# The last batch of a two-layer graph network without its list and its scatter: h gathered row by row, a plain product by chunks of rows, each chunk stored at once

## The chip, the cores and the metric

The kernel runs on one core of one Trainium2 chip. The time is the device time of one execution, in microseconds (us). A run lists that time, the core's span in the records and the mean clock that TensorE was granted. With one core no run is marked slow here; all runs below count as fast.

The traces name the engines PE (TensorE, matrix products and transposes; PEld are its weight loads), DVE (VectorE, sums and statistics), ACT (ScalarE, copies and activations), POOL (GpSimd, which issues the gathers) and SP (which issues plain transfers). A q behind the name, as in SPq, stands for the engine's queue of instructions. The granted clock is TensorE's: 1.00 is full, 0.50 half.

## The reference

There are 32 batches of x[512, 512], one adjacency matrix adj[512, 512], everything in float32, and two layers, each with a residual:

```python
h = jnp.maximum(_layernorm(x, axis=-1), 0.0)
x = x + (einsum('nm,bmd->bnd', adj, h) @ W0 + b0)                 # layer 0
h = jnp.maximum(_layernorm(x, axis=-1), 0.0)
# layer 1: eight heads of attention with the mask (1.0 - adj) * -1e9, then @ Wo + bo
x = x + gnn1(h, adj)
```

The mask is so strong that, with these inputs, each row's softmax has weight 1 at the largest entry of its row of adj and 0 elsewhere. The kernel checks this on the chip and otherwise takes a general path, which plays no part here. So layer 1 is: for every row take one row of h (by an index that all batches share), multiply it with Wv·Wo, and add a constant row.

## The kernel before

Fewer than 384 different rows of h are ever taken. So layer 1 gathers the list of used rows (`listed`, three times 128), multiplies those 384 rows only, writes the product z to DRAM, and lets a gather with addition bring z's rows to their places in x. Of the 384 rows, 256 go through a product form with seven half-size products in place of eight, the other 128 through a plain one.

```python
    def get_h(b):                                   # h has been written to DRAM as HS[b]
        HC[b] = work.tile([P, R, D], F32, name="hc")
        for r in range(R):
            nc.gpsimd.indirect_dma_start(
                out=HC[b][:, r, :], out_offset=None, in_=HS[b],
                in_offset=bass.IndirectOffsetOnAxis(ap=listed[:, r:r + 1], axis=0))
    ...
    def layer1(b):
        ...                                         # plain product of rows 256 to 383 into flat
        nc.vector.tensor_add(zs[:, 2, :], flat, cvo)
        nc.sync.dma_start(Z[b][2 * P:3 * P, :], zs[:, 2, :])
        yield from product(HT[b], HTS[b], wvo, wvo_t, take_z(zs, b), P)   # seven products, z written at the end

    def finish(b):
        for c in range(C):
            nc.gpsimd.indirect_dma_start(
                out=X[b][:, c, :], out_offset=None, in_=Z[b],
                in_offset=bass.IndirectOffsetOnAxis(ap=place[:, c:c + 1], axis=0), compute_op=ALU.add)

    def store(b):
        for c in range(C):
            nc.sync.dma_start(out[b, c * P:(c + 1) * P, :], X[b][:, c, :])
```

The batches are interleaved: while TensorE works on layer 0 of batch b, layer 1 of batch b-1 is fed, and batch b-2 is added and stored. Only at the end does a batch stand alone: batch 31 goes through gather, product, z, gather-add and store with nothing beside it but the end of batch 30.

## Time and profile before

| | us |
|---|---|
| median of the first three runs | 1216.17 (1215.86 to 1218.9) |
| the profiled run: span in the records | 1217.6 |
| the same run: its time (not one of the three) | 1219.35 |
| TensorE busy, share of the span | 96% |
| end of TensorE's last work to end of span | 24.6 |

The last line is the one that the change is about. The third line is the one to keep an eye on: a run's time is a little more than its own span. The profile's lines of the last batch stand in the prediction.

One line more is needed below, because the two kernels are compared from a common point: the first write of batch 31's h to DRAM, on SP's queue. Up to there their instructions are the same. In the kernel before (instructions in order of time; start, length):

```profile
1165.39 2.41 SPq L450 DMA_DIRECT2D hs<-h  x2
```

From this point to the end of the span are 1217.6 - 1165.39 = 52.2 us. I call this stretch the tail, and times in it are written as +n us after that point.

### The profile page before, as it was taken

How to read it: one execution, taken by the hardware profiler on the slowest of the kernel's cores; microseconds unless marked ns; L12 is line 12 of the kernel's file. 1: busy time of each engine (PE TensorE's matmuls, PEld its weight loads, DVE VectorE, ACT ScalarE, POOL GpSimd, SP SyncE). 2: the span in 40 equal slices, each digit the busy share in tenths (PEclk: the TensorE clock that was granted, in tenths of full speed). 3: DMA queues.
4: the chain of work that ended last, by engine and by line, in shares of the span. 5: the costliest groups of instructions: out<-in, count | busy, mean ns of one | idle time of the engine just before them, and what ended most of it. 6: DMA issues, size and time to landing. Idle time of an engine off the chain costs nothing.

```text
span 1217.6 us, 14536 instructions
## 1 busy us (share of the span) xinstructions
PE 1164.6 (96%) x5164; PEld 938.2 (77%) x5164; DVE 849.0 (70%) x1854; ACT 327.3 (27%) x499; POOL 401.9 (33%) x340
## 2 busy tenths in 40 slices
PE   7899999999999999999999999999999999999971
PEld 3458888888888888888888888888888888888841
DVE  4877776777777677777767777777777777777541
ACT  3223223222322322232232223223222322322110
POOL 1132432433233343324324332433433243343332
PEclk9999999999999999999999999999999999999986
DMA  8222665565566556556655655665565566555466
GB/s 284 78 61 91 169 169 147 152 188 167 152 169 167 149 152 186 169 152 167 167 149 152 185 170 152 168 168 148 152 186 170 153 166 171 144 152 153 135 162 149
DMA packets 97874, 192.43 MB, mean 158 GB/s; under 512 B 10624, under 2 KB 10624, under 8 KB 97792
## 3 DMA queue, kind: packets, MB, share of 16 engines
q1 hardware_dynamic: 69104, 127.95, 28.7%
q0 software_dynamic: 26528, 59.27, 26.6%
q10 hardware_dynamic: 2160, 4.19, 0.9%
q8 instruction: 42, 0.69, 0.2%
q14 instruction: 40, 0.33, 0.1%
HBM read 99.10 MB, written 92.28 MB: 157 GB/s over the span
## 4 chain that ended last, share of the span: by engine, by line
PE 86%; DVE 7%; DMA 1%; issue 1%; POOL 1%; ACT 0%; SPq 0%; POOLq 0%; DVEq 0%; ACTq 0%
PE mm L271 72%; PE mm L478 9%; PE pt L464 3%; DVE st L185 2%; DVE zs L482 2%; PE mm L352 1%; DVE zs L318 1%; DVE mv L186 1%; DMA hc<-hs,listed 1%; POOL x L488 0%; DMA z<-zs 0%; DVE x L422 0%; ACT h L199 0%; DVE x L445 0%; DVE yT L308 0%
## 5 line engine op out<-in xcount | busy, mean ns | idle before, releaser
L488 POOL DMA_INDIRECT x<-z,place x128 | 201.5, 1574 | 252.0 <-DMA z<-zs 209.6
L199 ACT ACTIVATE h<-x,off,rstd 128x512 f32<-128x512 f32 x256 | 194.7, 807 | 201.9 <-DVE off L195 201.9
L326 DVE TENSOR_TENSOR x<-mm,x 128x512 f32<-128x512 f32 x217 | 149.8, 690 | 119.1 <-PE mm L271 119.1
L192 POOL TENSOR_TENSOR rstd<-ve,mhalf 128x2 f32<-128x2 f32 (+1 forms) x97 | 88.2, 909 | 288.4 <-DVE ve L191 287.0
L185 DVE BATCH_NORM_STATS2 st<-x 128x6 f32<-128x512 f32 x256 | 175.3, 685 | 10.9 <-DMA x<-in_x_dram 8.7
L455 POOL DMA_INDIRECT hc<-hs,listed x96 | 102.8, 1071 | 235.3 <-PE mm L271 177.5
L271 PE MATMUL mm<-adjT_s,h0s 128*128 128x256 f32 x744 | 171.0, 379 | 3.8 <-DVE h0s L248 3.2
L271 PE MATMUL mm<-w_t,sel 128*128 128x256 f32 x744 | 171.0, 379 | 1.2 <-DVE x L326 1.2
L271 PEld LDWEIGHTS mm<-adjT_s,h0s 128*128 128x128 f32 x744 | 141.2, 190 | 23.6 <-issue 4.5
L271 PEld LDWEIGHTS mm<-w_t,sel 128*128 128x128 f32 x744 | 138.9, 190 | 19.1 <-DVE x L326 1.6
L465 ACT COPY hT<-pt 128x512 f32<-128x512 f32 x96 | 56.5, 588 | 356.3 <-PE pt L464 356.3
L310 ACT COPY yT<-mm 128x512 f32<-128x512 f32 x124 | 72.7, 586 | 266.2 <-PE mm L271 222.1
L478 PE MATMUL mm<-wvo,hT 128*128 128x512 f32 x256 | 116.8, 599 | 0.7 <-ACT hT L465 0.7
L271 PE MATMUL mm<-adjT,h 128*128 128x256 f32 x496 | 117.3, 379 | 0.0
L271 PE MATMUL mm<-w_s,yT 128*128 128x256 f32 x496 | 117.2, 379 | 0.0
L308 DVE TENSOR_TENSOR yT<-mm,yT 128x512 f32<-128x512 f32 x93 | 64.3, 692 | 75.2 <-PE mm L271 72.9
L271 PE MATMUL mm<-wvo_t,hTs 128*128 128x256 f32 x384 | 104.2, 395 | 6.5 <-DVE zs L318 6.2
L271 PEld LDWEIGHTS mm<-w_s,yT 128*128 128x128 f32 x496 | 94.2, 190 | 13.2 <-issue 0.5
L271 PEld LDWEIGHTS mm<-adjT,h 128*128 128x128 f32 x496 | 94.1, 190 | 13.3 <-ACT h L199 0.6
L271 PEld LDWEIGHTS mm<-wvo_t,hTs 128*128 128x128 f32 x384 | 67.9, 189 | 32.5 <-DVE zs L318 24.9
L478 PEld LDWEIGHTS mm<-wvo,hT 128*128 128x128 f32 x256 | 49.2, 193 | 49.5 <-issue 46.9
L422 DVE TENSOR_TENSOR x<-x,b_r 128x512 f32<-128x512 f32 x128 | 87.3, 683 | 0.0
(131 smaller groups left out, 1309.1 us busy)
## 6 DMA issues: line engine op xcount, KB each, us to landing
hs<-h SPq DMA_DIRECT2D x64, 512.0 KB
out_dram<-x SPq DMA_DIRECT2D x128, 256.0 KB
x<-in_x_dram SPq DMA_DIRECT2D x120, 256.0 KB
z<-zs SPq DMA_DIRECT2D x96, 256.0 KB
x<-z,place POOLq DMA_INDIRECT x128
hc<-hs,listed POOLq DMA_INDIRECT x96
x<-in_x_dram ACTq DMA_DIRECT2D x4, 256.0 KB
mask<-in_adj_dram SPq DMA_DIRECT2D x4, 256.0 KB
```

The costliest lines, as they stand in the source:

```text
L185: self.nc.vector.bn_stats(st, self.src[:, self.chunks[i], :])
L192: self.nc.gpsimd.tensor_tensor(self.rstd, ve, self.mhalf[:, 0:n], ALU.pow)
L199: self.nc.scalar.activation(self.dst[:, c, :], self.src[:, c, :], AF.Relu, bias=self.off[:, i:i + 1], scale=self.rstd[:, i:i + 1])
L271: nc.tensor.matmul(bank[:, m, :], lhs[:, k, m * P:(m + 1) * P], rhs[:, k, :], start=(first and m == 0 and k == 0), stop=(k == 1), skip_gro ...
L308: nc.vector.tensor_add(dst, bank, dst)
L310: nc.scalar.copy(dst, bank)
L326: nc.vector.tensor_add(dst, bank, dst)
L422: nc.vector.tensor_add(X[b][:, c, :], X[b][:, c, :], b0_r)
L455: nc.gpsimd.indirect_dma_start(out=HC[b][:, r, :], out_offset=None, in_=HS[b], in_offset=bass.IndirectOffsetOnAxis(ap=listed[:, r:r + 1], ...
L465: nc.scalar.copy(HT[b][:, :, r * P:(r + 1) * P], pt)
L478: nc.tensor.matmul(flat, HT[b][:, d, 2 * P:3 * P], wvo[:, d, :], start=(d == 0), stop=(d == DC - 1))
L488: nc.gpsimd.indirect_dma_start(out=X[b][:, c, :], out_offset=None, in_=Z[b], in_offset=bass.IndirectOffsetOnAxis(ap=place[:, c:c + 1], axi ...
```

## The change

The last batch pays for the detour over z with latency that nothing hides. So it takes the direct way: each of its 512 rows of h is gathered by its own index, four gathers in place of three; each chunk of 128 rows is transposed, multiplied by a plain product and added to x at once (the constant row has been added to x earlier), and its store leaves at once. This is more work for TensorE (512 rows in plain form in place of 384 with a cheaper one) and removes the write of z and the four gather-adds. The stores of batch 30 move to ACT's queue, so that SP's is free for the last batch.

```diff
+    def get_all(b):
+        for c in range(C):
+            nc.gpsimd.indirect_dma_start(
+                out=hs[0][:, c, :], out_offset=None, in_=HS[b],
+                in_offset=bass.IndirectOffsetOnAxis(ap=idx[:, c, 0:1], axis=0))
... (transpose_all: four transposes into one bank, one copy on ACT; add_cvo: x += cvo on DVE)
+    def layer1_rows(b):
+        transpose_all(0)
+        for r in range(C):
+            bank = ps_m.tile([P, D], F32, name="mm")
+            for d in range(DC):
+                if d == 2 and r + 1 < C:
+                    transpose_all(r + 1)
+                nc.tensor.matmul(bank, hs[1][:, d, r * P:(r + 1) * P], wvo[:, d, :], start=(d == 0), stop=(d == DC - 1))
+            nc.vector.tensor_add(X[b][:, r, :], bank, X[b][:, r, :])
+            nc.sync.dma_start(out[b, r * P:(r + 1) * P, :], X[b][:, r, :])
...
-        for b in range(B + 2):
+        for b in range(B + 1):
...
-            put(b, 13 if b > 0 else 16, get_h)
+            put(b, 13 if b > 0 else 16, get_h if b < B - 1 else get_all)
+            if b == B - 1:
+                for c in range(C):
+                    put(b, 22, add_cvo, c)
...
+        layer1_rows(B - 1)
+        if B > 1:
+            store(B - 2, nc.scalar)
```

More of the change, by code (lines that the diff above doesn't have):

```diff
@@ L457, in get_h, with transpose_all, add_cvo @@
                 in_offset=bass.IndirectOffsetOnAxis(ap=listed[:, r:r + 1], axis=0))
+    def get_all(b):
[3 more added lines that the diff above has]
+                in_offset=bass.IndirectOffsetOnAxis(ap=idx[:, c, 0:1], axis=0))
+    def transpose_all(r):
+        pt = ps_t.tile([P, DC, P], F32, name="pt")
+        for d in range(DC):
+            nc.tensor.transpose(pt[:, d, :], hs[0][:, r, d * P:(d + 1) * P], ident)
+        nc.scalar.copy(hs[1][:, :, r * P:(r + 1) * P], pt)
+    def add_cvo(b, c):
+        nc.vector.tensor_add(X[b][:, c, :], X[b][:, c, :], cvo)
+    def layer1_rows(b):
+        transpose_all(0)
+        for r in range(C):
+            bank = ps_m.tile([P, D], F32, name="mm")
+            for d in range(DC):
+                if d == 2 and r + 1 < C:
[3 more added lines that the diff above has]
+            nc.sync.dma_start(out[b, r * P:(r + 1) * P, :], X[b][:, r, :])
     def transpose_h(b, r):
@@ L490, in finish, with store @@
                 in_offset=bass.IndirectOffsetOnAxis(ap=place[:, c:c + 1], axis=0), compute_op=ALU.add)
-    def store(b):
+    def store(b, eng=nc.sync):
         for c in range(C):
-            nc.sync.dma_start(out[b, c * P:(c + 1) * P, :], X[b][:, c, :])
+            eng.dma_start(out[b, c * P:(c + 1) * P, :], X[b][:, c, :])
     def run(steps, work_by_step):
@@ L525, in single_path @@
                 put(b + 1, i, h0_sum, i)
-            for r in range(R):
+            for r in range(R if b < B else 0):
                 put(b - 1, 3 + r, transpose_h, r)
@@ L546, in single_path @@
             put(b, 11, put_h, 2)
-            put(b - 2, 12, store)
-            put(b, 13 if b > 0 else 16, get_h)
-            for step, i in ((11, 0), (11, 1), (12, 2), (12, 3)):
+            if b < B:
+                put(b - 2, 12, store)
+            put(b, 13 if b > 0 else 16, get_h if b < B - 1 else get_all)
+            if b == B - 1:
+                for c in range(C):
+                    put(b, 22, add_cvo, c)
+            for step, i in ((11, 0), (11, 1), (12, 2), (12, 3)) if b < B else ():
                 put(b - 1, step, hT_sum, i)
@@ L595, in single_path @@
             else:
-                run(layer1(b - 1) if b - 1 < B else None, todo[14:23])
+                run(layer1(b - 1) if b < B else None, todo[14:23])
+        layer1_rows(B - 1)
+        if B > 1:
+            store(B - 2, nc.scalar)
 @with_exitstack
```

## The prediction

> **What bounds the kernel now.** I read the page first (clock row, chain by engine), then the chain of waits in order of time over the last 120 us, then the instructions in order of time over the last 50 us, then the DMA view of the last 12 us, because the diff touches only the last batch, 31 of 0 to 31, and the store of batch 30.
>
> ```profile
> span 1217.6 us, 14536 instructions
> PEclk9999999999999999999999999999999999999986
> ...
> PE 86%; DVE 7%; DMA 1%; issue 1%; POOL 1%; ACT 0%; SPq 0%; POOLq 0%; DVEq 0%; ACTq 0%
> ```
>
> The reader is to see that TensorE sets the time of the whole, but not of the end: its granted clock falls only in the last two slices. Thirty-one batches are left as they are; the question is what the last 45 us are worth. The chain there:
>
> ```profile
> 1168.30 2.01 PE mm L271 x8
> ...
> 1170.98 1.04 POOL hc L455
> 1172.02 0.30 issue
> 1172.33 6.39 DMA hc<-hs,listed
> 1178.72 0.14 issue
> 1178.86 2.13 PE pt L464 x8
> ...
> 1181.64 5.28 PE mm L478 x8
> 1186.92 6.06 PE mm L271 x28
> ...
> 1193.44 1.63 SPq L483
> ...
> 1195.63 4.53 DMA z<-zs
> ...
> 1206.52 1.54 POOL x L488
> ```
>
> Columns: start, length (us), what. The last batch is a ladder of waits: gather the compacted rows of h (landed at 1178.72), transpose, product (ended at 1192.98), write z to DRAM (landed at 1200.16), gather-add z into x by four indirect transfers of POOL (1200.99 to 1208.06), then the stores. So 24.6 us of the span (1192.98 to 1217.6) have no TensorE work at all. The instructions in order of time show two details:
>
> ```profile
> 1193.00 0.42 DVE L318 TENSOR_TENSOR zs<-mm,cvo 128x256 f32<-128x256 f32 x1 [0.44 <-PE mm L271]
> 1193.18 1.89 SPq L483 DMA_DIRECT2D z<-zs  x1
> 1195.16 0.88 SPq L320 DMA_DIRECT2D z<-zs  x2
> 1200.99 1.54 POOL L488 DMA_INDIRECT x<-z,place  x1 [12.94 <-DMA z<-zs]
> ...
> 1206.09 6.96 SPq L494 DMA_DIRECT2D out_dram<-x  x4
> ```
>
> First, the z write at 1193.18 was ready at 1187.65 (its add, line 482, ran 1186.96 for 0.69); it stood behind the four stores of batch 30 on SP's in-order queue, which wait for that batch's gather-adds. Second, the last store was issued by 1213.05. The DMA view of 1206 to 1218, slices of 0.3 us, shows traffic until about 1214.7:
>
> ```profile
> DMA  9899869699999999999997400795000000000000
> ```
>
> So from the last data to the end of the span there are 2.9 us, which any version pays; and from the last gather-add's landing (about 1212, where the gap in this row lies) to the last data, 2.5 us for one 256 KB store.
>
> **What the Trainium skill says.** "DMA: Bandwidth & Descriptors", section "SWDGE vs HWDGE vs iDMA": per-element accumulation in a DMA is for GpSimd's software path only. The trace agrees: line 488 is POOL's, 1.54 us each plus 0.30 between, 7.1 us for four before the last one moves its data. Same page, "Issuing engines are not separate DMA queues": moving an issue to another engine saves only sequencer time, as all run on the same 16 DMA engines. I read the move of batch 30's store to ACT that way: it unblocks SP and makes no bandwidth. "Perfetto Trace Analysis", section "DMA Instruction — SWDGE (GPSIMD)": the profiled end is the end of descriptor generation, not of the data. Here the second gather shows about 1 us, and lands 6.4 us after its start. "TensorE: Matmul & The Clock Gate", Part 1: the clock halves after about one idle window of 3.4 us, and recovers after a busy one. The trace agrees:
>
> ```profile
> 1175.00:1178.00 3.00, 0.63 (x4) 0.42 (x4) 0.00 (x0) 0.59 (x1) 0.00 (x0) 1.00 0.87 283
> 1178.00:1185.00 7.00, 5.47 (x12) 2.94 (x13) 1.52 (x4) 1.17 (x2) 3.69 (x3) 0.51 0.29 50
> 1185.00:1190.00 5.00, 5.00 (x21) 3.61 (x19) 1.97 (x4) 0.00 (x0) 2.75 (x2) 1.00 0.96 176
> ```
>
> (After the stretch's length: busy time of PE, PEld, DVE, ACT, POOL; then granted clock, DMA share, GB/s.) While TensorE waits for gathers its clock goes to 0.51 and the eight matmuls of 128x512 take 5.28 us instead of the 3.43 us that the chain shows for them elsewhere.
>
> **The change part by part**, all for the last batch. The instruction orders of the two kernels agree on every engine up to there.
>
> Removed on the path: the z write (1193.0 to 1200.2, 7.2 us), the POOL gather-adds with their landing (1200.2 to about 1212, 11.8 us). Together 19 us. Also gone: four hTs sums, on DVE and not on the path.
>
> Added to the product: the seven-product form on 256 rows plus a plain one on 128 took 3.43 + 6.06 = 9.5 us warm (11.3 us here, cold at first). The plain product over all 512 rows is 16 matmuls of 128x512; each is two instructions at 0.43 us (3.43 us over 8), so 16 x 0.86 = 13.7 us. Transposes: four groups of 0.44 us. TensorE work 15.5 us against 10.8: 4.7 us more.
>
> Given back by starting earlier: before, the first matmul waits for all three gathers, 1181.64. After, it waits for the first only. First transposes at 1175.5 as before, ACT copy 0.59, first matmul at about 1176.85. Two steps of chunk 0 (1.7 us) run to 1178.6; then the second gather is needed, which landed at 1178.7. I take the same. From there TensorE has 3 x 0.44 + 14 x 0.86 = 13.4 us left: end at 1192.1, if warm. The third and fourth gathers are needed at about 1182.6 and 1186.5. The fourth is 256 KB more; issued around 1174.9 (spacing 1.3 us), it lands by my estimate at 1180 to 1181, as the whole traffic of gathers and z before (1.57 MB) moved from 1172.9 to about 1179, some 258 GB/s. So it's hidden.
>
> Added at the end: last DVE add 0.2 + 0.69, then the store 2.5, then the fixed 2.9: 6.3 us after TensorE's end, in place of 24.6. End at 1198.4 if warm. If the clock drops at 1177.9 as before, one window at half rate costs at most (1181.3 - 1178.7) / 2 = 1.3 us, two windows 3.0 us. In the window 1174.5 to 1177.9 TensorE is now busy about 1.7 us instead of 0.63, so I hold one window or none as likely as each other: +0.7 us on average.
>
> Added off the path: four adds of cvo to x on DVE (0.69 each, about 2.5 us in a row) stand ahead of the last take of batch 30, so the last z write of that batch goes out at about 1175.4 instead of 1173. Its landing (before: about 1179.9) then hardly moves, since the queues were full to 1179, but by up to 1 us it may. Batch 30's gather-adds start at 1180.7 to 1181.7 and take 7.1 us to the last issue and 4 to 5 us to land: 1192 to 1193. Its stores sit on ACT behind the fourth transpose copy (1187.6); the last is issued near 1193, lands 1195.5, and ends the span at 1198.4 too. Two paths that end together, and with batch 31's first three stores (0.75 MB) in the same stretch, where DMA was already 0.96 busy: I add 0.5 us for the later of two.
>
> Sum: 1198.4 + 0.7 + 0.5 = 1199.6 us of span. The profiled span was 1217.6 and the median time 1216.2, 1.4 less: 1198.2 us, a gain of 18 us, 1.5%.
>
> **The rivals.** (a) Batch 30's gather-adds become the end: z of batch 30 delayed, three more stores in their traffic, the store on ACT late. For: the 0.96 DMA share at 1185 to 1190, and the same landing time as the other path. Against: the gather-adds are paced by POOL's 1.84 us each, at 256 KB 142 GB/s. If they lose 3 us: 1201. (b) The clock: TensorE waits chunk by chunk for gathers, stays half-clocked for two windows, and all of the last batch's additional 4.7 us shows: 1201 to 1202. Against: a continuous stream of matmuls from 1178.7 should free it. (c) The best case: the later z write of batch 30 leaves the queues to the gathers, the second lands before 1178.6, and TensorE never waits after its first matmul: 1176.85 + 16 x 0.86 + 3 x 0.44 = 1191.9, + 6.3 = 1198.2, and 1.4 less as a time: 1196.8 with neither allowance. (d) The whole is hidden: no, nothing lies beside the 24.6 us.
>
> **Range and chances.** 1198.2 us; 1195 to 1202 holds rivals (a) to (c) and the run-to-run spread of 3 us. Faster by over 2% needs below 1192.3, that is, TensorE done by about 1187 in span, and its work alone from 1176.85 takes 15 us: 0.03. Within 2%: 0.96. Slower by over 2% would need a gather that collides with everything: 0.01.
>
> **What would show it.** TensorE's last matmul at 1191.5 to 1195; the span's end 6 to 7 us after it; no z write or gather-add of batch 31; first wvo matmul near 1177; the fourth gather landed before its transposes at 1186; clock in 1178 to 1182 either 1 or half. I'm wrong if TensorE waits for the second or later gathers beyond 1180, if the last chunk's store is not within 1 us of the last data, or if batch 30's stores end clearly after batch 31's.

## The result, and the profile after

| | before | after |
|---|---|---|
| median of four runs, us | 1217.54 (1215.86 to 1219.99) | 1202.93 (1201.75 to 1203.37) |
| profiled run: span, us | 1217.6 | 1201.6 |
| tail, us | 52.2 | 33.6 |
| mean granted clock | 0.988 | 0.996 |

The ratio is 0.9877, with a 95% interval of 0.986 to 0.9894: 1.2% less time, within 2%. A ratio here is the mean time of one kernel's fast runs over that of the other's in the same rounds, so it is not quite the ratio of the medians that stand beside it. The class came as predicted, the median did not: it lies 0.9 us above the range, and 4.7 us above the predicted 1198.2.

The page of the kernel after, span, clock row and chain by engine:

```profile
span 1201.6 us, 14516 instructions
PEclk9999999999999999999999999999999999999999
PE 88%; DVE 7%; DMA 1%; ACT 0%; issue 0%; POOL 0%; POOLq 0%; DVEq 0%; ACTq 0%
```

The two last slices no longer show a lowered clock, and SPq has left the chain. The chain in order of time shows a ladder with fewer rungs (start, length, what):

```profile
1173.60 4.34 DMA h<-hs,idx
1177.94 0.14 issue
1178.08 0.64 PE pt L468 x4
...
1179.38 1.98 PE mm L481 x4
1181.37 0.06 issue
1181.43 0.63 PE pt L468 x4
1182.06 3.44 PE mm L481 x8
...
1189.80 5.17 PE mm L481 x12
```

From the first product on, TensorE waits for nothing: the second, third and fourth gathers never appear, and eight instructions take 3.44 us, the rate of full clock. TensorE ends at 1194.97. The queues, from the instructions in order of time:

```profile
1168.01 0.37 SPq L450 DMA_DIRECT2D hs<-h  x1
...
1183.33 1.59 POOL L514 DMA_INDIRECT x<-z,place  x1 [4.91 <-ACT h L469]
1184.53 11.51 SPq L483 DMA_DIRECT2D out_dram<-x  x4
1189.90 6.38 ACTq L520 DMA_DIRECT2D out_dram<-x  x4
```

The first line is the common point. Batch 30's first gather-add, at 1183.33, is +15.3, as before (1180.70, also +15.3). The last stores leave on SP at 1196.04 and on ACT at 1196.28: two paths that end together. The DMA view of 1190 to 1202, in slices of 0.3 us:

```profile
DMA  8999999999999999998436989952200000000000
```

A 0 in this row is a share below a tenth. In slices of 0.2 us the data flow fully until about 1198.0, then there is a trickle, at 31 GB/s or less from 1198.8, until 1199.8; in the kernel before there is next to nothing after 1214.6, 3.0 us before the end. Set side by side, counted from the common point:

| step | predicted | measured |
|---|---|---|
| first transposes | 1175.5, +10.1 | 1178.08, +10.1 |
| first product | 1176.85, +11.5 | 1179.38, +11.4 |
| end of TensorE | 1192.1, +26.7 | 1194.97, +27.0 |
| end of span, with the allowances of 1.2 | 1199.6, +34.2 | 1201.6, +33.6 |

The tail was right to 0.6 us, and this profile kept the full clock in its tail, so that the 0.7 allowed for the clock fell away. So the 5.2 us between 1198.2 and this run's time of 1203.37 lie elsewhere: the common point itself comes 2.62 us later (1168.01 against 1165.39) in code that the diff doesn't touch; the tail is 0.62 us shorter than predicted; and this run's time is 1.77 us above its span where I had put it 1.4 below, 3.17 us. Indeed 2.62 - 0.62 + 3.17 = 5.17.

Where do 2.6 us go in untouched code? The stretch from 55 to 60 us shows it (length, busy time of PE, PEld, DVE, ACT, POOL, then granted clock, DMA share, GB/s). Before, then after:

```profile
55.00:60.00 5.00, 4.63 (x24) 4.01 (x24) 4.63 (x17) 2.00 (x3) 0.51 (x2) 1.00 0.54 210
```

```profile
55.00:60.00 5.00, 5.00 (x16) 3.94 (x15) 3.16 (x14) 2.00 (x3) 0.38 (x2) 0.50 0.54 210
```

In the setup the clock of the kernel after is 0.50 for a while: 16 matmuls instead of 24 in the same 5 us. Just ahead of it TensorE waits for sums on DVE, equally long in both (before, then after):

```profile
53.23 1.96 PE L271 MATMUL mm<-adjT_s,h0s 128*128 128x256 f32 x8 [3.16 <-DVE h0s L248]
```

```profile
53.10 2.49 PE L271 MATMUL mm<-adjT_s,h0s 128*128 128x256 f32 x8 [3.15 <-DVE h0s L248]
```

The same wait was followed by full clock once and by half clock once. By the weight product at 67 us the kernel after is 2.7 us late (it starts at 70.08 instead of 67.39), though its product after the wait started 0.13 us earlier.

### The profile page after: what moved, and what is told of

Read it like the earlier page. It is cut to its first block, busy times and chain, and to the rows that moved or that the text cites. A ratio compares the mean times of both kernels' runs of the same rounds, so it can differ in the third digit from the quotient of the medians.

```text
span 1201.6 us, 14516 instructions
## 1 busy us (share of the span) xinstructions
PE 1169.3 (97%) x5164; PEld 938.7 (78%) x5164; DVE 848.7 (71%) x1850; ACT 327.6 (27%) x500; POOL 396.4 (33%) x337
## 4 chain that ended last, share of the span: by engine, by line
PE 88%; DVE 7%; DMA 1%; ACT 0%; issue 0%; POOL 0%; POOLq 0%; DVEq 0%; ACTq 0%
PE mm L271 73%; PE mm L504 9%; PE pt L490 3%; DVE st L185 2%; DVE zs L508 2%; PE mm L481 1%; PE mm L352 1%; DVE zs L318 1%; DVE mv L186 1%; ACT h L199 0%; DMA h<-hs,idx 0%; DVE x L422 0%; DMA hs<-h 0%; DVE x L445 0%; PE pt L468 0%
## 5 line engine op out<-in xcount | busy, mean ns | idle before, releaser
L514 POOL DMA_INDIRECT x<-z,place x124 | 195.1, 1573 | 237.1 <-DMA z<-zs 196.8
L455 POOL DMA_INDIRECT hc<-hs,listed x93 | 99.6, 1071 | 232.4 <-PE mm L271 200.6
L504 PE MATMUL mm<-wvo,hT 128*128 128x512 f32 x248 | 111.5, 592 | 0.0
L271 PE MATMUL mm<-wvo_t,hTs 128*128 128x256 f32 x372 | 101.3, 395 | 6.5 <-DVE zs L318 6.2
```

The source lines that it names most:

```text
L271: nc.tensor.matmul(bank[:, m, :], lhs[:, k, m * P:(m + 1) * P], rhs[:, k, :], start=(first and m == 0 and k == 0), stop=(k == 1), skip_gro ...
L455: nc.gpsimd.indirect_dma_start(out=HC[b][:, r, :], out_offset=None, in_=HS[b], in_offset=bass.IndirectOffsetOnAxis(ap=listed[:, r:r + 1], ...
L504: nc.tensor.matmul(flat, HT[b][:, d, 2 * P:3 * P], wvo[:, d, :], start=(d == 0), stop=(d == DC - 1))
L514: nc.gpsimd.indirect_dma_start(out=X[b][:, c, :], out_offset=None, in_=Z[b], in_offset=bass.IndirectOffsetOnAxis(ap=place[:, c:c + 1], axi ...
```

## The experiments

Theories. First, a draw: whether the 3.15 us wait costs a stretch of half clock differs from run to run of one and the same program, and all four runs of the kernel after happened to have it. Rival: the change shifts something early in the program, so that its half clock comes always and the kernel before's never. For the tail, the open points were the queue of batch 30's stores, its traffic, and the clock in the waits for gathers. Every run below was timed in five rounds; each group of four shares a chip and the runs of the kernel before. Letters in the texts on record stand for the theories as those texts give them, and e1 to e4, e5 to e8, e9 to e12 and e13 to e16 are the runs of the four groups (e13 and e14 are told under the first), each in the order below. Where a "filler" is named, it is this, a few matmuls whose result nobody reads:

```python
def keep_warm(n):
    pt = ps_t.tile([P, DC, P], F32, name="pt")
    for i in range(n):
        nc.tensor.matmul(pt.rearrange("p c q -> p (c q)"), ones, adjT[:, i, :], start=True, stop=True)
```

### First group: is the early half clock drawn or made?

The kernel before once more, without an edit.

> The kernel before, unchanged, run again to get the span and granted clock of each of its runs. Theory L (lottery): the profile of the changed kernel lost 2.7 us between 53 and 63 us, in code that the change does not touch, because the granted clock fell to half for 6.8 us there; [...]some runs of the kernel before have it too: its runs fall in two groups some 2 to 3.5 us apart, the slower with the lower mean clock. Theory S (systematic): the changed program causes it and the kernel before never has it: one group, spread under 1 us.

Measured: 1218.98 us (13 runs, 1217.08 to 1220.79), ratio 1.0007; the shared runs of the kernel before had a median of 1218.16 (25 runs, 1215.53 to 1220.71). This time its own profile had the early stretch, at a clock of 0.67:

```profile
50.00:55.00 5.00, 3.89 (x13) 3.31 (x14) 3.90 (x11) 2.66 (x5) 1.33 (x2) 0.67 0.27 105
```

Over the 38 runs, the 22 with a mean clock of 0.986 or less took 1219.14 us on average, the 12 with 0.988 or more 1217.30. So one binary has both, and the rival's "never" is gone. It also says that the median of three on which I built, 1216.17, was a low one.

The kernel after once more, without an edit.

> The changed kernel, unchanged. L: most runs at a mean clock near 0.996 and 1201 to 1203.5 us, but with enough runs one or two near 0.999 and 1199 to 1200 us. S: all of them at 0.996 and 1201.5 to 1203.5 us. Both: ratio to the kernel before 0.986 to 0.989.

Measured: 1201.06 us, ratio 0.9855 (0.984 to 0.9871). The four runs fall into two groups: 1199.78 and 1200.31 at a clock of 0.998, 1201.8 and 1202.2 at 0.995 and 0.996. By that clock "always" is gone as well, though all four kept profiles of this kernel have the half clock.

Both kernels with the filler in the wait.

```diff
+                put(0, 8, lambda b: keep_warm(3))
```

> The kernel before plus three 128x512 matmuls into a PSUM tile that nothing reads, in TensorE's 3.2 us wait near 50 us for the sums of the first rows (3 x 0.86 = 2.6 us, so they should not delay what follows). L: its runs that had the early half clock lose it, the median falls by 0 to 2 us, to 1215.5 to 1217. S: no change, ratio 1.000.

> The changed kernel with the same three matmuls. L and S both: the early half clock goes, and the time falls by 2.5 us to 1199 to 1200.5 us; the profile shows the clock at 1.00 from 50 to 65 us and a span near 1198.5. Then the ratio to the kernel before with the same filler is the change's own worth: 1 - 17.5/1216.5 = 0.9855. If the half clock was not the cause of the missing 3 us, it stays at 1202 to 1203.

Measured: before with the filler 1216.27 us (13 runs), ratio 0.9989 (0.9981 to 0.9998); after with the filler 1199.92 us (1199.5 to 1200.47), ratio 0.9851. The early stretch of the latter:

```profile
55.00:60.00 5.00, 5.00 (x25) 4.41 (x24) 4.90 (x17) 0.44 (x1) 0.00 (x0) 1.00 0.27 105
```

Full clock, and the level of the fast pair of the run before; the four runs now spread by 1.0 us instead of 2.4. With both kernels filled, the change is worth 0.9851 / 0.9989 = 0.9862, 1.4%. The two ratios of the kernel after, 0.9855 without and 0.9851 with the filler, do not differ beyond their intervals; the profiles below tell more. The kernel before's spread hardly shrank (1214.76 to 1219.06), so the early wait isn't its only source.

Two more sets of the kernel after on another chip, to count the draws:

> The changed kernel again, to count half-clock runs. Shared draw: of 4 or more runs one to three have a mean clock of 0.997 or above and a time of 1199.5 to 1200.5 us, the others 0.995 to 0.996 and 1201.5 to 1203.5. Made more likely by the change: all at 0.995 to 0.996.

> The same again, same expectation; together with e13 some eight more runs.

Measured: 1202.01 us (0.9874) and 1200.94 us (0.9869). Three of four runs in each had the lower clock of 0.995 or 0.996. Over all 16 plain runs of the kernel after that makes 12 (4, 2, 3 and 3); of 87 runs of the kernel before in these calls, 56 had 0.987 or less. The boundary in the second count is only a guide, as the kernel before has a second half-clock stretch in its tail. One run of the last set had 0.996 and yet 1200.55 us, so the clock's mean sorts the runs only roughly. Still, both kernels draw the half clock often. The mean of the 16 plain runs of the kernel after is 1201.6 us; of the four medians, 1201.06 and 1200.94 lie in my range, 1202.01 on its edge, and 1202.93 above it.

The 18 kept profiles of all groups show the size more closely than the times. From the start of the product after the wait (53.23 and 53.10 in the two lines above) to the common point it is 1112.1 to 1112.4 us in 13 of them: the twelve with the filler and the first one of the kernel before. It is 1114.7 to 1114.9 us in the other five: the kernel before in this group and all four plain ones of the kernel after. These five have a half clock there, of 6.8 us in one stretch (the first two profiles of the kernel after) or of 3.4 us in each of two, the second between 65 and 70 us. So the early half clock costs 2.4 to 2.8 us in either kernel. With the filler the second stretch is absent too, although the filler doesn't lie there; why, stays open.

What else moves the common point is there before the wait: the product after it starts at 51.1 us in one profile and at 53.2 us in another. The two first profiles, at 53.23 and 53.10, were both late, so this cancels between them; between other runs it doesn't, and it is as large as most differences in the groups below.

### Second group: the queue of batch 30's stores, its traffic, and the order of the transposes

The filled kernel after, with batch 30's stores on SP ahead of the last batch's:

```diff
-        layer1_rows(B - 1)
         if B > 1:
-            store(B - 2, nc.scalar)
+            store(B - 2)
+        layer1_rows(B - 1)
```

> The changed kernel with the filler (as e4), but batch 30's four stores back on SP, ahead of the last batch's four. Theory Q (the queue matters): SP holds the last batch's finished chunks behind batch 30's last gather-add, which landed near the same time as TensorE's end; four stores of 0.6 us issue then stand between, so the end moves by 1 to 2.5 us: 1201 to 1202.5 us. Theory D (only the DMA engines matter, the issuing queue does not): within 0.5 us of e4's 1199.9.

Measured: 1200.56 us (five runs, 1199.82 to 1203.4), ratio 0.9881 on a chip whose kernel before is 1.2 us faster than the first group's. From SP's queue:

```profile
1183.98 6.95 SPq L520 DMA_DIRECT2D out_dram<-x  x4
1191.03 2.60 SPq L483 DMA_DIRECT2D out_dram<-x  x4
```

The last batch's first three stores wait for all of batch 30's, until 1191.03, and yet the tail is 34.06 us against 34.25 for the version with ACT, both with a half clock in the tail: the last store, which alone counts, isn't held up. In this pair the move to ACT is worth nothing. But two of the five runs took 1203.29 and 1203.4 us, while none of the 17 runs of the filled kernel after with the stores on ACT, with one filler or both, took more than 1200.69; no profile of such a run was kept. So that the queue never matters is not shown.

The other way round: the filled kernel before, with only batch 30's stores moved to ACT.

```diff
+        eng = nc.scalar if b == B - 2 else nc.sync
         for c in range(C):
-            nc.sync.dma_start(out[b, c * P:(c + 1) * P, :], X[b][:, c, :])
+            eng.dma_start(out[b, c * P:(c + 1) * P, :], X[b][:, c, :])
```

> The kernel before with the filler (as e3), and only batch 30's stores moved from SP to ACT. Q: the z write of the first rows, ready 5.5 us before SP gets to it, leaves at once, so the last z write, its landing and the gather-adds come about 2 us earlier: 1214 to 1215 us against e3's 1216.3, ratio 0.997 to 0.998. D: 1216.3, no change.

Measured: 1215.21 us (21 runs), ratio 0.9986 (0.9979 to 0.9992), where the filler alone had 0.9989 on the first chip. The gain that I expected didn't come. The block of z whose write stood behind those stores now leaves at 1187.04, +23.4 instead of +27.8 in the kernel before, but the last gather-adds wait for the whole of z, and its last blocks leave only when the product has ended; the gather-adds start at +33.4, with the filler alone at +32.9. The two profiles are no clean pair: here the half clock of the tail lasted 10.2 us instead of 6.8, the product ended at +28.7 instead of +27.3, and from its end to the gather-adds it was 4.7 us instead of 5.7. So 1 us of gain may be hidden by the clock; the times show none.

The filled kernel after, with all four chunks transposed before the first product.

```diff
-        transpose_all(0)
+        for r in range(C):
+            transpose_all(r)
...
-                if d == 2 and r + 1 < C:
-                    transpose_all(r + 1)
```

> The changed kernel with the filler (as e4), but the last batch's four chunks are all transposed before its first product, so TensorE waits for the fourth gather as the kernel before waited for its third. If the early start by chunks is worth what the prediction put it at, TensorE's first product starts about 4.5 us later and its end comes 2.5 to 4 us later (the transposes are no longer between products, the clock may fall): 1202 to 1204 us. If batch 30's own end sets the time and not TensorE, under 1 us: 1200 to 1201.

Measured: 1203.51 us (1203.0 to 1203.69), ratio 0.9894. Its chain:

```profile
1178.34 2.94 PE pt L468 x12
1181.28 14.94 PE mm L480 x32
```

The first product comes at +16.4 instead of +11.4, the end of TensorE at +31.3 instead of +28.4. So starting with one chunk, the part of the change that makes its longer product bearable, is worth about 3 us (1203.51 against the 1200.56 of the run before, on the same chip). Of the 5 us at the start 2.1 come back: 1.3 because three groups of transposes no longer lie between the products; the rest I put down to the clock in the two tails (half for 6.8 us here, for 3.4 us there), without having shown it.

The filled kernel after without any gather-add and store of batch 30. Its result is wrong on purpose (that batch's output stays unwritten).

```diff
-            put(b - 2, 1, finish)
+            if b < B:
+                put(b - 2, 1, finish)
...
-        if B > 1:
-            store(B - 2, nc.scalar)
```

> Wrong result on purpose: the changed kernel with the filler (as e4), without batch 30's gather-adds and stores. If TensorE's last product and the store after it set the end, and the traffic of batch 30 costs nothing: 1199.5 to 1200. If the two ends collide on the DMA engines as the prediction's allowance of 0.5 us said: 1199 to 1199.5. If batch 30's end is the later one or the traffic costs more than I think (rival a): 1197 to 1198.5, and the last data of the last batch's store lands 2.5 us or less after its issue.

Measured: 1201.42 us (1200.85 to 1201.86), ratio 0.9879, no better than with batch 30's end. The end comes 5.9 us after the start of the last add on DVE, with batch 30's traffic 5.84. With TensorE at half clock in the tail, as in both of these profiles, batch 30 costs nothing; my rival (a) didn't come about. The profiled run is slower by 0.4 us in the tail, which I can't explain, and by 0.7 us ahead of it, which was there already when the product after the early wait started (52.10 against 51.44); it is on another chip than the version that it undoes.

### Third and fourth group: the clock in the tail, and a better version

The filled kernel after again, as base on this chip:

> The same kernel as e4, to tie this chip to the others. 1199.5 to 1201.5 us, ratio 0.985 to 0.988; in its tail one half-clock window of 3.4 us, as in e4, e5 and e8.

Measured: 1200.02 us, ratio 0.9854. Then two fillers ahead of the last batch's first transposes, in the wait for the first gather.

```diff
+        keep_warm(2)
         layer1_rows(B - 1)
```

> As e9, plus two 128x512 matmuls that nobody reads in TensorE's last wait of 2.5 us, between batch 30's last product and the first gather. If the clock of the tail is a second lottery, it stays at 1.00 up to the end of the last product and the time falls by 1 to 1.7 us against e9, to about 1198.5 to 1199.5 us. If the clock window has nothing to do with that wait, no change.

Measured: 1199.79 us, ratio 0.985. The clock did what was wanted, from 0.66 to 1.00 in the stretch of 1174 to 1179 (base, then with the fillers):

```profile
1174.00:1179.00 5.00, 4.33 (x12) 1.92 (x11) 0.00 (x0) 0.59 (x1) 0.29 (x2) 0.66 0.61 193
```

```profile
1174.00:1179.00 5.00, 3.40 (x15) 1.92 (x15) 0.70 (x2) 0.87 (x2) 0.95 (x1) 1.00 0.82 274
```

The last add starts at +26.8 instead of +28.5. Yet the span ends at +33.2 instead of +34.2, and the median moved by 0.2 us: my expectation of 1 us or more was missed in the median. The two profiles show why it tells little: the tail is 1.0 us shorter, but the product after the early wait started 1.2 us later in the second (52.68 against 51.45), a draw that the change has no part in. The end comes 6.4 us after the start of the last add now, instead of 5.7. So with full clock something other than the last chunk's product has a say; batch 30's last store, issued by +26.9, is the suspect.

The same idea in the kernel before, two pairs of fillers in its waits for gathers:

```diff
+            if b == B:
+                todo[2].append(lambda: keep_warm(2))
+                todo[3].append(lambda: keep_warm(2))
```

> The kernel before with the early filler (as e3) and two pairs of unread matmuls in the last two waits for gathers. The last product runs in 9.5 us instead of 11.3, and the transposes before it in half their time: 2 to 2.7 us less than e3's 1216.3, 1213.5 to 1214.5 us. Then e10 against this one is the change's worth with the clock full on both sides: 15 to 16 us, 1.25 to 1.3%; if the tail's clock does not set the end of the kernel before, e11 stays at 1216.

Measured: 1216.58 us (13 runs), ratio 0.9991, no change from 0.9989 with the early filler alone. The fillers missed: a wait stayed partly empty, the clock from 1179 to 1184 was 0.66, and the eight matmuls of the plain product took 5.29 us, as in the kernel before. So this run doesn't tell what a full clock would be worth there.

A version meant to be best: both fillers, the adds of the constant row moved behind batch 30's last z write, and the last chunk's product, add and store in two halves of 256 columns.

```diff
+        for c in range(C):
+            add_cvo(B - 1, c)
         layer1_rows(B - 1)
... (in layer1_rows)
+            width = D if r + 1 < C else HALF
+            for first in range(0, D, width):
+                cols = slice(first, first + width)
```

> A version meant to beat both: as e10, with the four adds of the bias row moved behind batch 30's last z write, and the last chunk's product, add and store cut into two halves of 256 columns. The z write leaves 2.5 us earlier (about 7.7 instead of 10 us after the last h store begins), so batch 30's gather-adds start 1 to 2 us earlier, which is worth 0 to 0.5 us, as e5 and e8 say that this path is not the later one; the halves save the difference of a 0.69 and a 0.42 us add and half a store's transfer, 0.3 to 0.6 us. Together 0.3 to 1 us below e10: 1197.8 to 1199 us.

Measured: 1199.23 us (1198.78 to 1200.17), ratio 0.9846 (0.9833 to 0.986), the result correct: better than the two kernels, and 0.4 us in the means below the version with both fillers. That 0.4 us is not clear of the noise (0.985, 0.9837 to 0.9864, for the other), and the profiles don't show it in the tail: 33.25 us against 33.18. The last z write of batch 30 leaves at +8.3 instead of +10.2, but its gather-adds start at +14.45 instead of +14.66: the delay that the change causes there is hidden, as I had predicted.

Both fillers once more on another chip, and then without batch 30's end (wrong on purpose, as above), to see whether that end sets the last microsecond at full clock:

> As e10 (both fillers), to compare with e16 on one chip: 1199.3 to 1200.3 us; in the profile the end comes 6.2 to 6.6 us after the start of the last add, against 5.7 to 5.8 in e4 and e9, whose product ended 1.7 us later.

> Wrong result on purpose: as e15, without batch 30's gather-adds and stores. If batch 30's stores set the end once TensorE is at full clock, the end comes 5.7 to 5.8 us after the start of the last add and the time falls by 0.5 to 0.9 us against e15; if TensorE's path ends last in both, no change, 6.2 to 6.6 us.

Measured: 1200.01 us (0.9862) and 1200.99 us (0.9862; runs from 1198.3 to 1201.14). The second is inconclusive: its profile drew a half-clock stretch in the tail in spite of the fillers, and then the end comes 5.9 us after the start of the last add, as in every profile of the new last batch with a half clock there (5.7 to 5.9). In those with full clock it comes 6.2 to 6.7 us after (6.6 in the kernel after's first profile, 6.5 in the first of these two). That fits a collision of some 0.7 us (means of 6.5 and 5.8) between the two paths that end together. The traces agree in part: with a half clock batch 30's last store on ACT was issued 1.6 us or more ahead of the last batch's, with full clock between 0.9 us ahead of it and 1.1 us behind. But no run here takes batch 30 away at full clock and shows its profile; this stays open.

## Why the prediction was right or wrong

**The tail: right, with some luck at its end.** The first gather landed when I said, the first product began at +11.4 (predicted +11.5), no later gather was waited for, TensorE ended at +27.0 (+26.7), and the rest after it was 6.6 us (6.3, and 0.5 for the collision). In that rest two errors offset. The last store of the kernel before was issued at 1212.7, so that from the last gather-add to the end it is 4.9 us and not 2.5 + 2.9, and the last add starts 0.02 us after TensorE's end and not 0.2: the sum should have been 5.6, as the 5.7 to 5.9 us of the profiles with a half clock bear out, and what I called the collision some 0.7 us or more. The saving of the tail is 52.2 - 33.6 = 18.6 us in the two first profiles, and 51.3 - 33.6 = 17.7 in the second pair; I had expected 18. The extra 4.7 us of TensorE work that I had counted were paid for, as worked out, by starting with one chunk: with all transposes first, TensorE ends 2.9 us later.

**Off the path: right.** The four adds of the constant row delay batch 30's z write, and not its gather-adds (+15.3 in both). The two paths ended together. The move to ACT "unblocks SP" in the trace, and no gain of it is shown: in the one profile without it the end is the same, though two runs of that version were some 3 us slower, and given to the kernel before alone it doesn't change the time.

**The clock in the tail: right in kind.** I held one stretch of half clock or none as equally likely, at up to 1.3 us. The correct versions that keep the change's order of transposes had tails of 34.1 to 34.3 with it in the profiles, and of 33.0 to 33.7 with full clock: it is worth about 0.8 us, less than 1.3. TensorE's own end moves by more than that, from about +26.9 to +28.4: the half clock came 0.3 to 1.1 us before the +12.5 that I had assumed, over work of the first chunk, and no wait for the second gather followed that could have absorbed part of it. What holds up the end at full clock is the open point above. Which of the two comes is again a draw: after nearly the same wait of 2.6 to 2.8 us the four plain profiles of the kernel after kept the full clock three times and lost it once, and in the last run of all it was lost after waits of 1.07 and 0.68 us with four transposes between.

**The step that failed: from a span to a time.** The sentence was: "The profiled span was 1217.6 and the median time 1216.2, 1.4 less: 1198.2 us". It compares one run's span with the median of other runs. Within one run the time is above its span, 1219.35 against 1217.6 before, 1203.37 against 1201.6 after, and 1.67 to 1.86 us in every run that I looked at. Both figures of the profiled run before were on record, and I didn't put them side by side. The term should have been +1.75, and the prediction 1199.6 + 1.75 = 1201.35. This is 3.2 of the 5.2 us. The low median of three made the wrong sign look plausible: a profiled run of 1219.35 beside runs of 1215.86 to 1218.9 was simply a slow one: its start-up was the latest of the 18 profiles and its tail the longest of the kernel before's five.

**The term that was missing: the early half clock.** I took the common point at 1165.39 from a profile that had no half clock in the setup. The clock row of the page is too coarse to show it, and I didn't look at the waits of the setup. The kernel after draws a half clock there in 12 of 16 runs by its mean clock, at about 2 us (1200.0 against 1202.0 in the pairs of the second set), and in all of the first four. In the profiles it costs 2.4 to 2.8 us, and 2.75 us in the first one of the kernel after, less the 0.13 by which that one was ahead. That is the other 2.6 us of that run, and it took the median just out of the range: 1201.35 was inside, 1202.93 is not. That the half clock hangs on the 3.15 us wait is shown by the filler: five of six profiles without it have the half clock, none of the twelve with it. What decides it in a given run, I only know to differ between runs of one binary.

**The base.** The 16 plain runs of the kernel after average 1201.6 us, and the runs of the kernel before some 1217.9: a gain of about 16 us, 1.3%, where I had named 18. With the early filler in both it is 16.7 us (1216.66 to 1199.95 in the means). The tail of the first profile before, 52.2, was the longest of five (with and without fillers, down to 49.9), so some of the 18 was a draw of that profile. One more sum of the prediction is off, without bearing on the result: 2% below 1216.2 is 1191.9, not 1192.3.

## What to carry to other kernels

When a predicted end of the span is turned into a time, use the profiled run's own time and span, never another run's median; and when the range is narrower than the spread between runs, look for waits of about 3 us anywhere in the program, not just in the part that changes, and compare profiles from common points, since here the start-up alone moved everything by up to 2 us. In the last stage of a pipeline, where nothing hides latency, a direct form with more work can beat a cheaper one with a detour: here 4.7 us more of TensorE bought the removal of about 19 us of write, gather-add and landing, provided that it starts with the first chunk of data. And where two paths end together, shortening one need not show in full: ending the last product 1.7 us earlier shortened the tail by 1.0 us.

## What the Trainium skill lacked or had wrong

- "TensorE: Matmul & The Clock Gate", Part 1, says that the window is free-running and that the number of cold matmuls at the start varies from run to run, at under 1% of a span. The runs agree with the size, but the page doesn't say that a wait in the middle of a program is such a draw too: after one and the same wait of 3.15 us the clock of 55 to 60 us was 1.00 in one profile and 0.50 in another, and the two profiles of the kernel before stood 2.7 us apart for it. Every stretch of half clock that these 18 profiles show between 50 us and the end of TensorE's work lasts 3.4, 6.8 or 10.2 us, in step with the page's window.
- "DMA: Bandwidth & Descriptors", section "Anatomy of one DMA", has a fit that gives, as an estimate, 2.6 us for 256 KB. In the last batch, at a DMA share of 0.87 (the kernel before, 1175 to 1178 us), gathers of 256 KB took more: 4.3 to 6.3 us from start to landing for the four of the kernel after, and 6.39 us for the second of the kernel before. The cost of a gather that adds stands on no page: on POOL 1.54 us, and 0.30 us between, for 256 KB, against about 1.0 us for a plain gather.
